# Masked attention with a group norm in front: two visits of each group of heads exchange places

## The chip, the cores and the metric

The kernel runs on one core of a Trainium2 chip. The metric is the device time of one launch in microseconds (us). The kernel before takes 1812.58 us, the median of three runs (1812.48, 1812.58 and 1813.05).

Engine names are those of the profile: PE is the matrix engine and PEld its weight loads, ACT the scalar engine, DVE the vector engine, POOL the GpSimd engine, SP the engine that only issues transfers here.

## The reference

`x` is 32 images of 256 channels and 32 x 32 pixels, float32. Each image goes through a group norm (32 groups of 8 channels), is projected to queries, keys and values (1x1 convolutions, that is, products with 256 x 256 weights), and attends over its own 1024 pixels with 8 heads of 32 channels. A pixel sees only the pixels before it (the diagonal is masked too). The input is added at the end.

```python
xf = _gn(x).reshape(B, C, S)                       # B=32, C=256, S=1024
q = jnp.einsum('oc,bcs->bos', q_w, xf) + q_b[None, :, None]
kv = jnp.einsum('oc,bcs->bos', kv_w, xf) + kv_b[None, :, None]
...
mask = jnp.tril(jnp.ones((S, S), dtype=x.dtype), -int(MASK_CENTER))
scores = jnp.einsum('bhqd,bhkd->bhqk', q, k) / jnp.sqrt(jnp.asarray(dk, x.dtype))
scores = jnp.where(mask == 0, jnp.asarray(-10000.0, x.dtype), scores)
attn = jax.nn.softmax(scores, axis=-1)
attn = jnp.where(mask == 0, jnp.asarray(0.0, x.dtype), attn)
out = jnp.einsum('bhqk,bhkd->bhqd', attn, v)
return x + out
```

## The kernel before, in words

**Visits.** The 1024 keys are eight blocks of 128, and so are the queries. The scores stand with keys on the partitions and queries along the row. The blocks at or below the diagonal (36 of 64) are worked off in six *visits* for each group of four heads; an image has two groups (`NG` = 2), so twelve visits, and the launch has 32 x 12 = 384 of them. `VISITS` (L557) says what a visit makes. Its long part goes to a tile `e` of 128 x 4 heads x 512, its short part to a tile `eh`. A short part is either a `pair` (the two diagonal blocks of two neighbouring key blocks, packed into 192 columns a head) or a plain piece of 256 columns (`full`). Visits 0, 1, 3 and 5 have a pair, visits 2 and 4 a plain piece. Visit 4 is the *visit of three pieces*: a long part of 384 and 128 columns, a short one of 256. Visit 5 has a long part of 512 columns and the diagonal pair of key blocks 4 and 5, which is `pair(2, 0)`.

**One turn of the loop (L705 to L722).** Turn i issues `scores` of visit i (L339), then what is listed for the turn in `at` (a projection of the next image, as a rule), then `values` of visit i-1 (L399), `add_keys` of visit i-1 (L421), and then what is listed in `after`. The order of the instructions on each engine is the order in which this code issues them (`manual_schedule`); an engine takes them strictly one after the other, and semaphores hold an instruction back until its inputs are there. The numbers of turns below are those inside an image, 0 to 11.

- `scores`: PE makes the score products (L302) into three double banks of PSUM. ACT takes the exponentials: two calls for `e` (L384), then one for `eh` (L380). If the visit is in `PAIRS`, `mask` (L320) is called at once: two `affine_select` on POOL (L330) turn the pair in `eh` into two masked squares in the tile `diagonal`, of which there is one for the first two pairs (tag "D", 0) and one for the last two ("D", 1).
- `values`: PE multiplies the exponentials with the values (L409), by the list `PRODUCTS` (L568). A product that reads "D" needs the mask of its pair. After the last visit of a half (visits 1 and 5) ACT copies the sum out (L418).
- `add_keys`: DVE adds the tiles of exponentials into one, by the list `ADDS` (L583), at L427. The sum of the second half is gathered in the long tile of visit 2 (`TOTAL`).

**What else goes by turns.** `PREPARE` (L624) spreads the norm of the next image over turns; for b of 2 and more it is called with the first visit of image b, so the offsets -12 to -3 fall in the image before. In turn 3 stand `norm_mean` (PE L162 into `pm`, ACT L185) and `norm_deviation`: three tiny `tensor_tensor` on DVE of 2 elements a partition each (L195, L196, L197), which make `dev`. In turn 4, after `values` and `add_keys`, stand `norm_variance` (PE: eight small products `pv` of `avg` and `dev`, L162; ACT: L209) and `norm_rstd` (POOL: L217, L219). `norm_apply` on ACT (L235) follows in turns 5, 6, 7 and 9.

`SUMS` (L625) has the folds of the summed exponentials: `fold` (L436) adds half of the partitions onto the other half, by a transfer that POOL issues (L440), in turns 3 and 5 for the first sum, 7 and 9 for the second, 10 and 12 (turn 0 of the next image) for the third, 13 and 15 for the fourth. `stack` (L442, SP) collects them, `sum_folded` (L448), `invert` (L485) and `finish` (L521) come an image later on DVE and SP.

**Buffers.** The tag "e" has four buffers, which the tiles take in turn: long tiles of visits 0, 1, 3, the second diagonal tile (made in visit 3), then those of visits 4 and 5. The tag "eh" has three. `acc` of PSUM has one.

**The last image** has no projection beside it and is not folded. `sums` (L466) adds the keys up on PE with a matrix of ones (`pd`, L461), by the list `SUMMED` (L595). Where a visit of the last image is in `SUMMED` (other than visit 1), `add_keys` is left out for it. At the very end PE makes the sums of visit 11 and its values, and DVE inverts and finishes in two halves (`end_last`, L536).

Of the kernel before, what the change touches and what calls it, by code (L numbers as in the profile page):

```python
# [17 lines left out]
P = 128  # L18
# [14 lines left out]
def tile_norm_attention_residual(  # L33
# [20 lines left out]
    B, C, H, W = x.shape  # L54
# [44 lines left out]
    def unshifted():  # L99
# [178 lines left out]
        def full(kb, first, width, at):  # L278

            return at, width, [[(c, kb, first, width, slice(at, at + width))] for c in (0, KEYS)]  # L280

        def pair(j, at):


            even, odd = 2 * j, 2 * j + 1
            c0, c1, c2, c3 = (at + n * KEYS for n in range(4))
            return at, 3 * KEYS, [
                [
                    (0, even, even * P, P, slice(c1, c3)),
                    (0, odd, odd * P, KEYS, slice(c0, c1)),  # L290
                ],
                [
                    (KEYS, odd, odd * P, P, slice(c0, c2)),
                    (KEYS, even, even * P + KEYS, KEYS, slice(c2, c3)),
                ],
            ]
# [23 lines left out]
        def mask(b, g, raw, j):  # L320


            hf, place = j // 2, (2 * j % 4) * P
            if ("e", b, g, "D", hf) not in live:
                live["e", b, g, "D", hf] = epool.tile(
                    [P, 4, HALF], F32, tag=("e0", "e")[hf], bufs=4, name=f"diagonal_{b}_{g}_{hf}"
                )
            square = live["e", b, g, "D", hf]
            for s in range(2):
                nc.gpsimd.affine_select(  # L330
                    out=square[:, :, place + s * P : place + (s + 1) * P],
                    in_=raw[:, :, (1 - s) * KEYS : (3 - s) * KEYS],
                    pattern=[[0, 4], [(1, -1)[s], P]], compare_op=ALU.is_gt, fill=0.0, base=0,
                    channel_multiplier=(-1, 1)[s],
                )
            if j == 0:
                nc.gpsimd.memset(square[0:1, :, 0:1], 1.0)

        def scores(b, v):  # L339
# [27 lines left out]
            for ins in first:  # L367
                tc.declare_no_dep(wait.ins, ins.ins, reason="the semaphore orders them")
            made = short_of((0, 1), *rest if i in PAIRS else ())
            if i not in PAIRS:  # L370
                for f in rest:
# [19 lines left out]
            live["e", b, g, "L", i], live["e", b, g, "H", i] = e, eh  # L391
            if i in PAIRS:
                mask(b, g, eh, PAIRS[i])

# [141 lines left out]
        def end_last(b):  # L536
# [4 lines left out]
            for part in both:  # L541
# [13 lines left out]
        Q = lambda a, b: slice(a * P, b * P)  # L555
# [3 lines left out]
            ([full(1, 2 * P, 4 * P, 0)], [pair(1, 0)]),  # L559
            ([full(0, 4 * P, 4 * P, 0)], [full(1, 6 * P, 2 * P, 0)]),  # L560
            ([full(2, 4 * P, 4 * P, 0)], [pair(3, 0)]),
            ([full(4, 5 * P, 3 * P, 0), full(6, 7 * P, P, 3 * P)], [full(5, 6 * P, 2 * P, 0)]),
            ([full(3, 4 * P, 4 * P, 0)], [pair(2, 0)]),
        ]
        N, TOTAL = NG * len(VISITS), 2
        PAIRS = {0: 0, 1: 1, 3: 3, 5: 2}

        PRODUCTS = [  # L568
            (0, [
# [3 lines left out]
            (0, [(("L", 1, Q(0, 2)), 1, Q(2, 4)), (("D", 0, Q(2, 3)), 2, Q(2, 3)), (("D", 0, Q(3, 4)), 3, Q(3, 4))]),  # L573
            (1, [(("L", 2, Q(0, 4)), 0, Q(0, 4)), (("L", 1, Q(2, 4)), 1, Q(0, 2)), (("H", 2, Q(0, 2)), 1, Q(2, 4))]),
            (1, [(("L", 3, Q(0, 4)), 2, Q(0, 4)), (("D", 1, Q(2, 3)), 6, Q(2, 3)), (("D", 1, Q(3, 4)), 7, Q(3, 4))]),
            (1, [
                (("L", 4, Q(0, 3)), 4, Q(1, 4)), (("L", 4, Q(3, 4)), 6, Q(3, 4)), (("H", 4, Q(0, 2)), 5, Q(2, 4)),
            ]),
            (1, [(("L", 5, Q(0, 4)), 3, Q(0, 4)), (("D", 1, Q(0, 1)), 4, Q(0, 1)), (("D", 1, Q(1, 2)), 5, Q(1, 2))]),
        ]  # L580
        FIRST, LAST = (0, 2), (1, 5)

# [2 lines left out]
            [(("D", 0, Q(1, 4)), ("L", 0, Q(0, 3))), (("D", 0, Q(2, 4)), ("L", 1, Q(0, 2)))],  # L585
            [(("L", 2, Q(0, 2)), ("L", 1, Q(2, 4))), (("L", 2, Q(2, 4)), ("H", 2, Q(0, 2)))],
            [(("L", 2, Q(0, 4)), ("L", 3, Q(0, 4)))],
            [
                (("L", 2, Q(1, 4)), ("L", 4, Q(0, 3))), (("L", 2, Q(3, 4)), ("L", 4, Q(3, 4))),
                (("L", 2, Q(2, 4)), ("H", 4, Q(0, 2))),  # L590
            ],
            [(("L", 2, Q(0, 4)), ("D", 1, Q(0, 4))), (("L", 2, Q(0, 4)), ("L", 5, Q(0, 4)))],
        ]

        SUMMED = {  # L595
            1: [(("D", 0, Q(0, 4)), Q(0, 4))],
            5: [(("L", 2, Q(0, 4)), Q(0, 4)), (("L", 5, Q(0, 4)), Q(0, 4)), (("D", 1, Q(0, 4)), Q(0, 4))],
            7: [(("D", 0, Q(0, 4)), Q(0, 4)), (("L", 0, Q(0, 3)), Q(1, 4)), (("L", 1, Q(0, 2)), Q(2, 4))],
            9: [(("L", 2, Q(0, 4)), Q(0, 4)), (("L", 3, Q(0, 4)), Q(0, 4))],
            10: [  # L600
                (("L", 4, Q(0, 3)), Q(1, 4)), (("L", 4, Q(3, 4)), Q(3, 4)), (("H", 4, Q(0, 2)), Q(2, 4)),
                (("D", 1, Q(2, 4)), Q(2, 4)),
            ],
            11: [(("L", 5, Q(0, 4)), Q(0, 4)), (("D", 1, Q(0, 2)), Q(0, 2))],
        }
        at, after = {}, {}

# [124 lines left out]
    def shifted():  # L732


        with ExitStack() as inner:
# [34 lines left out]
            with tc.For_i(0, B, 1) as b:  # L770
# [93 lines left out]
                )  # L864

    outside = unshifted()
    again = nc.values_load(outside[0:1, 0:1], min_val=0, max_val=P)
    with tc.If(again > 0):
# [26 lines left out]
```

## Time and profile before

| what | value |
|---|---|
| median of three runs | 1812.58 us |
| the profiled execution | 1813.86 us |
| its span, first to last instruction | 1812.2 us |
| busy: PE, DVE, ACT, POOL | 1797.5, 1643.0, 1457.2, 919.4 us |
| mean granted clock of PE | 0.999 |
| score products L302, 18432 of them | 584.9 us busy |
| value products L409 from `e` and `diagonal` (4608 and 4096 of them) | 401.8 and 160.4 us busy |
| `affine_select` L330, 512 of them | 649.1 us busy, 1291 ns mean |
| additions `e<-e,diagonal` of 2048 elements, L427, 62 of them | 142.1 us busy, 2293 ns mean |

A row of the view of groups gives line, engine, operation, tiles, shapes and count, then busy time and the mean duration of one, then the idle time of the engine just before them and what ended it. In the timeline a row has start and duration in us from the span's beginning, and in square brackets the idle time before it with its releaser. In the list of waits the figures are us in total, times, and the longest.

An image takes about 55.45 us in the steady part: the starts of the first score products of images 5 and 6 differ by that, as those of most other neighbours do.

### The profile page before, as it was taken

The page shows a single profiled execution, that of the slowest core. Times are in us where ns is not written, and L with a number is a line of the kernel's source. Part 1 is how long each engine was busy: PE and PEld are TensorE (multiplying, and loading weights), DVE is VectorE, ACT ScalarE, POOL GpSimd, SP SyncE. Part 2 cuts the span into 40 slices and gives each one's busy share as a digit, 9 for nine tenths or more (in the row PEclk, how much of TensorE's full clock was granted, in tenths as well). Part 3 has the DMA queues.
Part 4 walks back from the last instruction along what each step waited for, and adds up shares of the span by engine and source line. Part 5 has one row for each costly group of instructions (what it writes and reads, how often), then busy time and mean ns, then how long its engine had stood idle before and what let it go on. Part 6 is the DMA issues. An engine that isn't in the chain of part 4 may idle for free.

```text
span 1812.2 us, 81732 instructions
## 1 busy us (share of the span) xinstructions
PE 1797.5 (99%) x37036; PEld 956.9 (53%) x37036; DVE 1643.0 (91%) x1832; ACT 1457.2 (80%) x1985; POOL 919.4 (51%) x901
## 2 busy tenths in 40 slices
PE   9999999999999999999999999999999999999997
PEld 5555555555555555555555555555555555555553
DVE  4689999999999999999999999999999999999987
ACT  6888878888778888788887888887888878888774
POOL 2345555545545555455555455554554555555532
PEclk9999999999999999999999999999999999999999
DMA  3457676776766766766767667677667676675653
GB/s 124 72 96 142 130 138 124 137 149 130 147 118 137 145 131 139 133 132 133 148 135 146 111 137 153 125 142 132 136 132 147 132 140 122 134 156 121 124 113 85
DMA packets 86531, 236.78 MB, mean 131 GB/s; under 512 B 21280, under 2 KB 22304, under 8 KB 70304
## 3 DMA queue, kind: packets, MB, share of 16 engines
q0 software_dynamic: 15872, 97.53, 35.8%
q1 hardware_dynamic: 70304, 133.96, 28.2%
q8 instruction: 290, 4.75, 1.1%
q14 instruction: 65, 0.53, 0.1%
HBM read 66.85 MB, written 34.57 MB: 56 GB/s over the span
## 4 chain that ended last, share of the span: by engine, by line
PE 98%; DVE 1%; ACT 0%; issue 0%; DMA 0%; POOL 0%; DVEq 0%
PE sT L302 30%; PE acc L409 27%; PE pp L162 26%; PE ppv L162 13%; PE pd L461 0%; ACT e L384 0%; PE pv L162 0%; DMA x<-in_x_dram 0%; DVE diagonal L427 0%; DVE st L177 0%; DVE e L427 0%; PE pm L162 0%; POOL diagonal L330 0%; ACT eh L380 0%; DVE rb_last L528 0%
## 5 line engine op out<-in xcount | busy, mean ns | idle before, releaser
L330 POOL TENSOR_SCALAR_AFFINE_SELECT diagonal<-eh 128x512 f32<-128x512 f32 x512 | 649.1, 1291 | 748.6 <-ACT eh L380 748.4
L384 ACT ACTIVATE e<-sT 128x1024 f32<-128x1024 f32 x768 | 745.2, 1022 | 260.7 <-PE sT L302 256.7
L302 PE MATMUL sT<-q,k 32*64 32x128 f32 (+2 forms) x18432 | 584.9, 372 | 0.5 <-issue 0.3
L427 DVE TENSOR_TENSOR e<-e,e 128x1024 f32<-128x1024 f32 x315 | 553.6, 1757 | 21.6 <-ACT v L266 4.8
L302 PEld LDWEIGHTS sT<-q,k 32*64 32x64 f32 x18432 | 405.4, 131 | 181.4 <-PE sT L302 59.3
L162 PE MATMUL pp<-xn,wT 128*32 128x512 f32 x4096 | 493.3, 598 | 0.6 <-issue 0.3
L409 PE MATMUL acc<-e,v 128*32 128x384 f32 (+3 forms) x4608 | 401.8, 450 | 0.0
L380 ACT ACTIVATE eh<-sT 128x768 f32<-128x768 f32 (+1 forms) x384 | 340.9, 888 | 0.0
L409 PEld LDWEIGHTS acc<-e,v 128*32 128x32 f32 x4608 | 149.7, 110 | 261.0 <-issue 238.0
L162 PE MATMUL ppv<-wT,xn 128*32 128x256 f32 x4096 | 247.5, 382 | 0.0
L162 PEld LDWEIGHTS pp<-xn,wT 128*32 128x32 f32 x4096 | 107.8, 109 | 200.1 <-issue 165.9
L427 DVE TENSOR_TENSOR diagonal<-diagonal,e 128x1536 f32<-128x1536 f32 x126 | 188.4, 1495 | 16.8 <-PE acc L409 9.1
L427 DVE TENSOR_TENSOR e<-e,eh 128x1024 f32<-128x1024 f32 x127 | 176.0, 1386 | 6.9 <-DVE e L427 0.5
L427 DVE TENSOR_TENSOR e<-e,diagonal 128x2048 f32<-128x2048 f32 x62 | 142.1, 2293 | 39.2 <-POOL diagonal L330 36.2
L409 PEld LDWEIGHTS acc<-diagonal,v 128*32 128x32 f32 x4096 | 119.6, 110 | 92.9 <-issue 75.7
L162 PEld LDWEIGHTS ppv<-wT,xn 128*32 128x32 f32 x4096 | 120.4, 109 | 79.6 <-issue 7.2
L409 PE MATMUL acc<-diagonal,v 128*32 128x128 f32 x4096 | 160.4, 273 | 0.0
L235 ACT ACTIVATE xn<-x,shift,rstd 128x256 f32<-128x256 f32 x248 | 137.1, 613 | 0.0
L440 POOL DMA_DIRECT2D e<-e x124 | 102.3, 825 | 38.1 <-PE pp L162 31.1
L528 DVE SCALAR_TENSOR_TENSOR rb<-num,v_bias_col,x 128x256 f32<-128x256 f32 x248 | 117.5, 514 | 4.4
L440 POOL DMA_DIRECT2D diagonal<-diagonal x124 | 119.4, 963 | 0.0
L526 DVE TENSOR_TENSOR num<-num,rb 128x512 f32<-128x512 f32 x124 | 110.8, 894 | 0.0
(78 smaller groups left out, 1004.4 us busy)
## 6 DMA issues: line engine op xcount, KB each, us to landing
diagonal<-diagonal POOLq DMA_DIRECT2D x62, 512.0 KB, 8.3
e<-e POOLq DMA_DIRECT2D x62, 512.0 KB, 5.2
rb<-inverses SPq DMA_DIRECT2D x124, 256.0 KB, 4.7
out_dram<-rb SPq DMA_DIRECT2D x124, 256.0 KB, 5.1
x<-in_x_dram SPq DMA_DIRECT2D x120, 256.0 KB, 6.2
diagonal<-diagonal POOLq DMA_DIRECT2D x62, 256.0 KB, 4.9
folded<-diagonal SPq DMA_DIRECT2D x62, 256.0 KB, 4.4
e<-e POOLq DMA_DIRECT2D x62, 256.0 KB, 5.1
```

The costliest lines, as they stand in the source:

```text
L162: nc.tensor.matmul(out[part], lhsT=lhsT[:, part], rhs=rhs, start=start, stop=stop, skip_group_check=True)
L235: nc.scalar.activation(to, of, AF.Identity, bias=live["shift", b][:, g : g + 1], scale=rstd)
L302: return nc.tensor.matmul(bank[c : c + KEYS, cols], lhsT=live["k", b, g][rows, kb * P + c : kb * P + c + KEYS], rhs=live["q", b, g][rows, ...
L330: nc.gpsimd.affine_select(out=square[:, :, place + s * P : place + (s + 1) * P], in_=raw[:, :, (1 - s) * KEYS : (3 - s) * KEYS], pattern=[ ...
L380: exp = nc.scalar.activation(eh.rearrange("p (n bank) q -> p bank n q", n=2)[:, :, :, :narrow], short[:, :, :, :narrow], AF.Exp)
L384: nc.scalar.activation(e[:, 2 * a : 2 * a + 2, :wide], pairs[a][:, :, :wide], AF.Exp)
L409: nc.tensor.matmul(acc[HD * j : HD * (j + 1), of], lhsT=live["v", b][:, kb, h * HD : (h + 1) * HD], rhs=e[:, j, :], start=first, stop=last ...
L427: nc.vector.tensor_add(to, to, tile_of(b, g, at))
L440: nc.gpsimd.dma_start(out=total[:rows], in_=total[rows : 2 * rows], accum_op=ALU.add)
L526: nc.vector.tensor_mul(num, num, rb)
L528: nc.vector.scalar_tensor_tensor(blocks(rb, s), blocks(num, s, s == 1), v_bias_col[:, g : g + 1], blocks(xt[:, g, cols], s), ALU.add, ALU.add,
```

## The change

The last two entries of `VISITS` exchange places. The pair of key blocks 4 and 5 (with the 512 columns of key block 3) becomes visit 4, the visit of three pieces becomes visit 5. The lists that go by visit follow: `PAIRS`, `PRODUCTS`, `ADDS` and `SUMMED`. `LAST`, `TOTAL`, `PREPARE`, `SUMS` and all other lists of turns stay as they are.

```diff
             ([full(2, 4 * P, 4 * P, 0)], [pair(3, 0)]),
+            ([full(3, 4 * P, 4 * P, 0)], [pair(2, 0)]),
             ([full(4, 5 * P, 3 * P, 0), full(6, 7 * P, P, 3 * P)], [full(5, 6 * P, 2 * P, 0)]),
-            ([full(3, 4 * P, 4 * P, 0)], [pair(2, 0)]),
         ]
...
-        PAIRS = {0: 0, 1: 1, 3: 3, 5: 2}
+        PAIRS = {0: 0, 1: 1, 3: 3, 4: 2}
...
+            (1, [(("L", 4, Q(0, 4)), 3, Q(0, 4)), (("D", 1, Q(0, 1)), 4, Q(0, 1)), (("D", 1, Q(1, 2)), 5, Q(1, 2))]),
             (1, [
-                (("L", 4, Q(0, 3)), 4, Q(1, 4)), (("L", 4, Q(3, 4)), 6, Q(3, 4)), (("H", 4, Q(0, 2)), 5, Q(2, 4)),
+                (("L", 5, Q(0, 3)), 4, Q(1, 4)), (("L", 5, Q(3, 4)), 6, Q(3, 4)), (("H", 5, Q(0, 2)), 5, Q(2, 4)),
             ]),
-            (1, [(("L", 5, Q(0, 4)), 3, Q(0, 4)), (("D", 1, Q(0, 1)), 4, Q(0, 1)), (("D", 1, Q(1, 2)), 5, Q(1, 2))]),
...
+            [(("L", 2, Q(0, 4)), ("D", 1, Q(0, 4))), (("L", 2, Q(0, 4)), ("L", 4, Q(0, 4)))],
             [
-                (("L", 2, Q(1, 4)), ("L", 4, Q(0, 3))), (("L", 2, Q(3, 4)), ("L", 4, Q(3, 4))),
-                (("L", 2, Q(2, 4)), ("H", 4, Q(0, 2))),
+                (("L", 2, Q(1, 4)), ("L", 5, Q(0, 3))), (("L", 2, Q(3, 4)), ("L", 5, Q(3, 4))),
+                (("L", 2, Q(2, 4)), ("H", 5, Q(0, 2))),
             ],
-            [(("L", 2, Q(0, 4)), ("D", 1, Q(0, 4))), (("L", 2, Q(0, 4)), ("L", 5, Q(0, 4)))],
...
-            5: [(("L", 2, Q(0, 4)), Q(0, 4)), (("L", 5, Q(0, 4)), Q(0, 4)), (("D", 1, Q(0, 4)), Q(0, 4))],
+            5: [
+                (("L", 2, Q(0, 4)), Q(0, 4)), (("L", 5, Q(0, 3)), Q(1, 4)), (("L", 5, Q(3, 4)), Q(3, 4)),
+                (("H", 5, Q(0, 2)), Q(2, 4)),
+            ],
...
-            10: [
-                (("L", 4, Q(0, 3)), Q(1, 4)), (("L", 4, Q(3, 4)), Q(3, 4)), (("H", 4, Q(0, 2)), Q(2, 4)),
-                (("D", 1, Q(2, 4)), Q(2, 4)),
-            ],
-            11: [(("L", 5, Q(0, 4)), Q(0, 4)), (("D", 1, Q(0, 2)), Q(0, 2))],
+            10: [(("L", 4, Q(0, 4)), Q(0, 4)), (("D", 1, Q(0, 4)), Q(0, 4))],
+            11: [(("L", 5, Q(0, 3)), Q(1, 4)), (("L", 5, Q(3, 4)), Q(3, 4)), (("H", 5, Q(0, 2)), Q(2, 4))],
```

## The prediction, made before the changed kernel was built

> **What bounds the kernel now.** I read the page first, then the list of waits, then the timeline of one image, engine by engine.
>
> ```profile
> span 1812.2 us, 81732 instructions
> ...
> PE 1797.5 (99%) x37036; PEld 956.9 (53%) x37036; DVE 1643.0 (91%) x1832; ACT 1457.2 (80%) x1985; POOL 919.4 (51%) x901
> ...
> PE 98%; DVE 1%; ACT 0%; issue 0%; DMA 0%; POOL 0%; DVEq 0%
> ```
>
> PE is busy for 99% of the span and carries 98% of the chain that ended last. So the time changes only where a PE product starts earlier or later. But the end of a matmul in the records is modelled, so a short wait of PE can hide inside "busy". I therefore measured starts, not busy time. The list of waits has two of the places where PE depends on other engines:
>
> ```profile
> PEld acc L409 <- POOL diagonal L337: 5.6, 28, 0.3
> ...
> PE pv L162 <- DVE dev L197: 0.6, 2, 0.4
> ```
>
> The first is turn 7: the values of visit 6 wait for the mask of its pair (the memset at L337 comes behind both selects). From the first product of `acc` to the next score product takes 1.548 us in 28 images, and 1.413 in images 0, 1 and 24, where the mask is early: 0.135 us each. The second is what matters here. Turn 4 of image 20 on PE:
>
> ```profile
> 1147.75 1.55 PE L302 MATMUL sT<-q,k 32*64 32x256 f32 x48
> 1149.23 1.93 PE L162 MATMUL ppv<-wT,xn 128*32 128x256 f32 x32
> 1150.98 1.04 PE L409 MATMUL acc<-e,v 128*32 128x512 f32 x8
> 1151.84 0.62 PE L409 MATMUL acc<-diagonal,v 128*32 128x128 f32 x16
> 1152.33 0.24 PE L162 MATMUL pv<-dev,avg 128*32 128x2 f32 x8
> 1152.50 1.47 PE L302 MATMUL sT<-q,k 32*64 32x128 f32 x48
> ```
>
> and DVE in the same place:
>
> ```profile
> 1150.50 1.21 DVE L427 TENSOR_TENSOR e<-e,eh 128x1024 f32<-128x1024 f32 x1
> 1151.64 0.15 DVE L195 TENSOR_TENSOR dev<-mv,mean 128x2 f32<-128x2 f32 x1
> 1151.82 0.16 DVE L196 TENSOR_TENSOR dev<-dev 128x2 f32<-128x2 f32 x1
> 1152.02 0.16 DVE L197 TENSOR_TENSOR dev<-dev,mv 128x2 f32<-128x2 f32 x1
> 1152.09 2.29 DVE L427 TENSOR_TENSOR e<-e,e 128x2048 f32<-128x2048 f32 x1
> ```
>
> `dev` is ready at 1152.18, `pv` starts 0.147 us later, and this 0.147 is the same in images 2 to 30: PE is waiting for DVE there, in 29 images. It costs nothing yet. In image 1 `dev` is done 1.9 us early, and `pv` starts 4.575 us after the turn began; in the others it is 4.58. So the slack is zero, and every delay of `dev` stops PE, with scores, projections and values of all later turns queued behind it.
>
> **The skill.** "SBUF — State Buffer", section "SBUF: two separate sides", says that DVE and GpSimd share a pair of ports under an exclusive lock: a DVE operation with two SBUF inputs and a GpSimd operation exclude each other, and the loser waits for the whole instruction of the other. The trace agrees, even for the smallest operation. In image 0 two selects meet the same `dev`:
>
> ```profile
> 27.15 1.67 POOL L330 TENSOR_SCALAR_AFFINE_SELECT diagonal<-eh 128x512 f32<-128x512 f32 x2 [5.55 <-ACT eh L380]
> ```
>
> ```profile
> 27.35 0.98 DVE L427 TENSOR_TENSOR e<-e 128x512 f32<-128x512 f32 x1 [12.20 <-PE acc L409]
> 28.25 0.58 DVE L195 TENSOR_TENSOR dev<-mv,mean 128x2 f32<-128x2 f32 x1
> 28.87 0.16 DVE L196 TENSOR_TENSOR dev<-dev 128x2 f32<-128x2 f32 x1
> ```
>
> L195, 147 ns elsewhere, takes 584 and ends with the second select (28.82). The two sides also alternate: select 1, addition, select 2, L195. A select takes 0.63 us alone and ends about 0.49 us after a lock it waited for. "Perfetto Trace Analysis", section "Tensor Engine Instruction (MATMUL, LD_WEIGHTS)", says that the end of a PE instruction is estimated and its start observed; the `pv` wait above, with no gap shown on PE, is such a case.
>
> **The change, part by part.** PE's work in an image is the same: 768 columns of values in both exchanged visits (1.408 us each), 1.403 us for the scores of a pair visit, 1.481 for three pieces. Turns 4 and 10 become 0.078 shorter, 5 and 11 as much longer. ACT's exponential of the short part (0.82 us for a pair, 1.03 for three pieces) moves by one visit; ACT is ready by the next scores in both orders. The DVE additions of turns 5 and 6 exchange (2 x 2048 against 1536 + 512 + 1024 elements). Each of these is hidden, and costs nothing unless a step below says so.
>
> *Step 1, the moved mask.* In turn 5 the exponential of the pair ends 3.85 us into the turn, and the first select starts at 3.92 (1156.42, turn from 1152.50). In turn 4 the same sequence will put it at 1147.75 + 3.92 = 1151.67. That is between L195 (1151.64) and L196 (1151.82), while the addition in front still holds the ports until 1151.71. POOL is free there (its last issue ends at 2.58 us of the turn). If L195 goes first, select 1 holds the ports to about 1152.28, L196 ends there, select 2, queued since then, to 1152.77, and L197 ends with it or just behind: 0.60 us late. If select 1 goes first (1151.71 to 1152.20), L195 slips in behind it, select 2 ends at 1152.70, then L196 and L197 to 1152.90: 0.72 late. I take the middle, 0.66. Bounds: 0 if all three `dev` operations get in before a select, 0.32 if L197 slips in between the two selects, 0.95 if each of the selects finds nobody and runs its full 0.63 with the gaps of DVE behind it. `pv` starts by the same amount later. The 0.078 that PE saves in the scores of turn 4 is lost, since `pv` waits; the 0.078 more in turn 5 is paid. So 0.74 us an image, 29 images: +21.5. Behind `pv` wait all of PE, ACT's L209, POOL's L217 and the norm; none of these is late by more than `pv` itself.
>
> *Step 2, the wait of turn 7 goes.* Both selects of visit 6 now meet two additions of 2048 (2.29 us) on DVE: 2.10 and 2.68 us for the two. After the change they meet 1536, 512 and 1024 (nominally 1.75, 0.69, 1.23). DVE reaches the 1536 about 3.4 us into turn 6; select 1 waits from 3.94 to its end (5.15), is done at 5.65, the 512 comes to 6.2, select 2 to 6.7, so 2.05 us into turn 7, where it is needed at 4.0. What is late next there is PE itself. 28 x 0.135: -3.8.
>
> *Step 3, the second group.* In turn 10 the mask queues behind the second fold on POOL (issue to 4.2 us) and an addition of 2048; DVE's next addition needs the mask and waits about 1 us. It must be back in step at turn 1, where its addition at L427 waits for PE at 4.11 us and DVE is free at 3.50. I find it free at about 3.85: 0, with an upper bound of 0.3 us an image. The fold of the third sum is issued some 3 us later, lands 8.3 us after that, before its successor at 2.5 us of turn 1: 0.
>
> *Step 4, the end.* The sums of turn 7 of the last image lose 256 of 1536 columns (1778.04 to 1780.72: 2.68 us in all): -0.43. The last sum no longer waits for a mask:
>
> ```profile
> 1798.70 1.04 PE L461 MATMUL pd<-e,pick 128*32 128x512 f32 x8
> 1800.00 0.64 PE L461 MATMUL pd<-diagonal,pick 128*32 128x256 f32 x8 [0.26 <-POOL diagonal L330]
> ```
>
> Without it the second row would start 0.87 after the first, 0.43 earlier; DVE, which goes on from there, had been idle for 0.42: -0.42.
>
> Sum: 21.5 - 3.8 - 0.43 - 0.42 = +16.8 us. The profiled execution was 1813.86 us (span 1812.2 and 1.7 around it), 0.07% above the median of 1812.58; the median plus the sum is 1829.4.
>
> **The rivals.**
> - *One select in between* (L197 before select 2): 0.40 x 29 = 11.6, sum +7.0, 1819.5 us. For it: L197 follows L196 by 0.04 us only. Against: in every meeting that I looked at, the waiting side got the ports next.
> - *No collision, on the other side*: the three tiny operations run through, and the selects come behind. Then turn 4 pays 0.078 x 29 = 2.3, and the rest stays: -2.3, 1810.3 us; if `dev` came another 0.08 earlier, 1808.0. It decides at 1152.18: a first select that gets the ports only after this harms nobody. For it: L195 is issued 0.03 before the select. Against: gaps of 0.03 between dependent operations, in which POOL already waits, and image 0.
> - *DVE out of step as well*: step 3 comes out at its upper bound, DVE is late at turn 1 by 0.3 us and with it `dev`: 28 x 0.3 = 8.4, about 1838 us. For it: DVE is 91% busy. Against: the free 0.6 us at turn 1.
> - *No effect where it was meant*, the wait at turn 7 stays since DVE is late by the delay of `pv`: 3.8 more, inside the range.
>
> **How the numbers follow.** Both selects in between 0.50, one 0.20, none 0.17, out of step 0.13. Range 1815 to 1841: it holds the first, the second and the fourth case. About 0.2%, 3.6 us, is what a measurement of this kernel can tell from no change. "None" gives -2.3 to -4.6, so I split it: faster 0.06, same 0.11, slower 0.83.
>
> **What would show it.** In the changed profile `pv` should start about 5.2 us after turn 4 began, 0.147 behind L197; L195 or L196 should last some 0.5 us and end with a select; the image should take about 56.05 us; the row of `acc` waiting for L337 should be gone, and the wait of `pd` for L330 too. If L195 to L197 keep their 0.15 us in all images, step 1 is wrong, and the time is below 1812. If `pv` is on time and the kernel is slower all the same, the cause is one that I have not named.

## The result, and the profile after

The changed kernel takes 1833.27 us, the median of four runs (1830.86 to 1834.68); the kernel before, beside it on the same chip, 1812.56 (1812.48 to 1813.05). The ratio is 1.0112, with a 95% interval of 1.0095 to 1.013. It is slower, by 20.7 us; 1829.4 had been predicted, with a range of 1815 to 1841. The profiled execution took 1833.38 us.

The head of the page after, with the chain that ended last by engine:

```profile
span 1831.7 us, 81670 instructions
...
PE 1798.4 (98%) x37036; PEld 961.7 (53%) x37036; DVE 1667.8 (91%) x1831; ACT 1454.9 (79%) x1985; POOL 780.6 (43%) x901
...
PE 93%; DVE 6%; issue 1%; ACT 0%; POOL 0%; DVEq 0%; POOLq 0%
```

The span grew by 19.5 us, and PE's busy time by 0.9 only: PE now stands still. The chain passes through DVE for 6% of the span instead of 1%. In the list of waits (us in total, times, longest), the row of `pv` has grown from 0.6 us:

```profile
DVE e L427 <- POOL diagonal L330: 36.8, 33, 1.1
...
PE pv L162 <- DVE dev L197: 16.4, 27, 1.1
```

The row of `acc` waiting for L337 is gone, as is that of `pd` waiting for L330. The first row here, DVE waiting for the mask of the second group, is not a new loss: in the kernel before it has 36.2 us, also in 33 waits. The exchange only moved it. 31 of these waits now fall in turn 11 by PE's count; before, they fell in turn 0 of the next image. No turn of PE is longer for it.

Turn 4 of image 20 of the changed kernel, on PE:

```profile
1158.68 1.48 PE L302 MATMUL sT<-q,k 32*64 32x128 f32 x48
1160.09 1.93 PE L162 MATMUL ppv<-wT,xn 128*32 128x256 f32 x32
1161.84 1.04 PE L409 MATMUL acc<-e,v 128*32 128x512 f32 x8
1162.70 0.62 PE L409 MATMUL acc<-diagonal,v 128*32 128x128 f32 x16
1163.98 0.24 PE L162 MATMUL pv<-dev,avg 128*32 128x2 f32 x8 [0.66 <-DVE dev L197]
```

on DVE:

```profile
1161.39 1.21 DVE L427 TENSOR_TENSOR e<-e,eh 128x1024 f32<-128x1024 f32 x1
1162.52 0.15 DVE L195 TENSOR_TENSOR dev<-mv,mean 128x2 f32<-128x2 f32 x1
1162.70 0.55 DVE L196 TENSOR_TENSOR dev<-dev 128x2 f32<-128x2 f32 x1
1163.29 0.55 DVE L197 TENSOR_TENSOR dev<-dev,mv 128x2 f32<-128x2 f32 x1
1163.76 2.28 DVE L427 TENSOR_TENSOR e<-e,e 128x2048 f32<-128x2048 f32 x1
```

and on POOL:

```profile
1162.61 1.22 POOL L330 TENSOR_SCALAR_AFFINE_SELECT diagonal<-eh 128x512 f32<-128x512 f32 x2 [1.39 <-ACT eh L380]
```

L195 still runs free. The first select starts 3.93 us into the turn, L196 waits for it and lasts 0.55 us instead of 0.16; the second select is queued meanwhile, and L197 waits for that one. `pv` starts 5.30 us into the turn, 0.14 behind the end of L197; before, it was 4.58. This isn't one image. The view by tile gives minimum, median and maximum over the launch (ns):

```profile
L196 DVE TENSOR_TENSOR dev<-dev x32: 160/547/554, 8.5 to 1728.0; 128x2 f32<-128x2 f32 x32
L197 DVE TENSOR_TENSOR dev<-dev,mv x32: 161/552/554, 8.7 to 1728.6; 128x2 f32<-128x2 f32 x32
L195 DVE TENSOR_TENSOR dev<-mv,mean x31: 146/149/585, 28.4 to 1727.8; 128x2 f32<-128x2 f32 x31
```

To see where the 19.5 us lie, I took the start of the first score product of each turn, and the median over images 2 to 30 of the distance to the next. Seven of the twelve turns are the same in both kernels to 0.001 us. The five others:

| us | turn 4 | turn 5 | turn 7 | turn 10 | turn 11 | all twelve |
|---|---|---|---|---|---|---|
| before | 4.753 | 4.552 | 4.692 | 4.630 | 4.563 | 55.449 |
| after | 5.476 | 4.630 | 4.558 | 4.552 | 4.640 | 56.114 |
| difference | +0.723 | +0.078 | -0.134 | -0.078 | +0.077 | +0.665 |

29 times 0.665 is 19.3. What images 2 to 30 last beyond 29 such medians, in single pauses of PE, is 4.6 us after and 3.4 before: +1.2. The last image is 1.0 shorter. These make the 19.5.

Below, the sum of the twelve medians is called the *steady image*, and the time beyond 29 of them *pauses*. All times below are of runs at a granted clock of 0.995 or more; one of the seven runs of the kernel with only the second group exchanged had 0.702, took 2424.36 us, and is left out.

### The profile page after: what moved, and what is told of

It is laid out like the page before. It is cut to its first block, busy times and chain, and to the rows that moved or that the text cites. A ratio compares the mean times of both kernels' runs of the same rounds, so it can differ in the third digit from the quotient of the medians.

```text
span 1831.7 us, 81670 instructions
## 1 busy us (share of the span) xinstructions
PE 1798.4 (98%) x37036; PEld 961.7 (53%) x37036; DVE 1667.8 (91%) x1831; ACT 1454.9 (79%) x1985; POOL 780.6 (43%) x901
## 3 DMA queue, kind: packets, MB, share of 16 engines
q8 instruction: 290, 4.75, 1.1%
## 4 chain that ended last, share of the span: by engine, by line
PE 93%; DVE 6%; issue 1%; ACT 0%; POOL 0%; DVEq 0%; POOLq 0%
PE sT L302 30%; PE pp L162 26%; PE acc L409 25%; PE ppv L162 10%; DVE e L427 3%; DVE dev L196 1%; DVE dev L197 1%; PE pd L461 1%; PE pv L162 0%; PE busy L148 0%; DVE rb L533 0%; ACT e L384 0%; DVE diagonal L427 0%; DVE dev L195 0%; PE pm L162 0%
## 5 line engine op out<-in xcount | busy, mean ns | idle before, releaser
L330 POOL TENSOR_SCALAR_AFFINE_SELECT diagonal<-eh 128x512 f32<-128x512 f32 x512 | 515.2, 1028 | 892.0 <-ACT eh L380 892.0
L409 PE MATMUL acc<-e,v 128*32 128x512 f32 (+3 forms) x4608 | 403.5, 450 | 0.0
L427 DVE TENSOR_TENSOR e<-e,eh 128x1024 f32<-128x1024 f32 x126 | 181.5, 1441 | 6.8 <-ACT xn L235 0.5
L440 POOL DMA_DIRECT2D diagonal<-diagonal x124 | 111.5, 899 | 64.3 <-DMA diagonal<-diagonal 64.3
```

Of the source, the lines that this page charges most:

```text
L330: nc.gpsimd.affine_select(out=square[:, :, place + s * P : place + (s + 1) * P], in_=raw[:, :, (1 - s) * KEYS : (3 - s) * KEYS], pattern=[ ...
L409: nc.tensor.matmul(acc[HD * j : HD * (j + 1), of], lhsT=live["v", b][:, kb, h * HD : (h + 1) * HD], rhs=e[:, j, :], start=first, stop=last ...
L427: nc.vector.tensor_add(to, to, tile_of(b, g, at))
L440: nc.gpsimd.dma_start(out=total[:rows], in_=total[rows : 2 * rows], accum_op=ALU.add)
```

## The experiments

The eleven kernels ran in three groups, each group on one chip and beside the kernel before, whose median there was 1814.2 to 1814.3 us (1812.0 to 1817.5). Ratios are to it; they and their intervals are estimates over the runs, not quotients of the medians.

| run | us, median (range) | ratio, 95% interval | profiled execution | steady image | pauses |
|---|---|---|---|---|---|
| first group only exchanged | 1839.19 (1834.95 to 1840.51) | 1.0137, 1.0121 to 1.0152 | 1834.95 | 56.115 | 5.5 |
| second group only | 1820.50 (1811.95 to 1822.25) | 1.0021, 1.0006 to 1.0037 | 1822.25 | 55.390 | 13.6 |
| `dev` ahead of the additions | 1818.40 (1815.65 to 1821.81) | 1.0025, 1.0019 to 1.0032 | 1817.80 | 55.380 | 10.3 |
| `dev` on ACT | 1811.99 (1806.57 to 1815.07) | 0.9979, 0.997 to 0.9988 | 1811.99 | 55.270 | 8.2 |
| before + two selects on `e` | 1835.71 (1835.35 to 1835.79) | 1.0117, 1.0102 to 1.0132 | 1835.72 | 56.266 | 1.9 |
| before + two selects on `eh` | 1834.38 (1832.58 to 1837.87) | 1.0112, 1.0098 to 1.0127 | 1834.90 | 56.203 | 1.9 |
| second group, earlier fold | 1824.45 (1820.37 to 1834.46) | 1.006, 1.004 to 1.008 | 1829.10 | 55.394 | 20.0 |
| `dev` on ACT, earlier fold | 1838.11 (1833.52 to 1849.64) | 1.0137, 1.0113 to 1.0161 | 1838.86 | 56.168 | 7.7 |
| first group, `dev` on ACT | 1837.01 (1832.47 to 1847.63) | 1.0132, 1.0108 to 1.0156 | 1837.53 | 56.194 | 5.8 |
| before, `dev` on ACT | 1823.55 (1820.48 to 1828.16) | 1.0053, 1.0038 to 1.0068 | 1824.45 | 55.641 | 8.2 |
| second group, no stores | 1809.06 (1808.62 to 1809.69) | 0.997, 0.9959 to 0.9981 | 1809.18 | 55.408 | 1.1 |

The last two columns are read from the profiled execution alone. Executions of one kernel differ by up to 16 us, and a profiled one can be far from typical: with the first group only it is the fastest of four, with the second group only the slowest of six.

### One group alone

The five lists were made per group of heads, and one group kept the old order.

```diff
-            longs, shorts = VISITS[i]
+            longs, shorts = VISITS[g][i]
...
-            if i in PAIRS:
-                mask(b, g, eh, PAIRS[i])
+            if i in PAIRS[g]:
+                mask(b, g, eh, PAIRS[g][i])
```

> The two visits exchange places in the first group of heads alone (visits 4 and 5); the second group keeps the order of before. Theory (the selects of the moved mask come between the three dev operations of turn 4, and pv with all of PE waits 0.72 us in 29 images): the loss stays whole, turn 4 takes 5.48 us, an image 56.11, about 1833.5 us. Rival A (the second group pays: the mask of turn 10 behind a fold on POOL, DVE waiting for it, late at turn 1): the loss goes for the most part, below 1818 us. Rival B (PE itself pays for the new order of its products, in either group): about half of the 20.7 us, near 1823.

> The exchange in the second group alone (visits 10 and 11). Theory: no dev operation near turn 10, so no loss; turn 7 keeps its wait of 0.135 us; 1812.0 to 1812.6 us, image 55.45. Rival A (second group): close to 1833. Rival B (PE's own order): near 1823.

With the first group exchanged the steady image is 56.115, with 5.476 in turn 4 and 4.558 in turn 7: the whole steady loss of the change lies here, and the gain at turn 7 too. The median lies 5.7 us above the 1833.5 that had been expected; the one execution with a trace, the fastest, has 5.0 us of pauses in turn 0. With the second group alone turn 4 is 4.749 and turn 7 still 4.637, so the steady image is 0.06 below before, worth 1.7 us. The kernel is slower all the same, by pauses of 6.5 us in turn 4 and 6.8 in turn 5. I had not foreseen these (the kernel before has 0.3 and 0.0 there); the last experiments below deal with them.

### The three small operations elsewhere

In the changed kernel, L195 to L197 go ahead of the two additions of visit 2 on DVE:

```diff
-                    if b < B - 1 or v not in SUMMED or v == 1:
+                    late = v == 2
+                    if not late and (b < B - 1 or v not in SUMMED or v == 1):
                         add_keys(b, v)
...
+                if i and late:
+                    add_keys(b, v)
```

> The changed kernel, with one thing reordered on DVE: in turn 3 the three dev operations are issued ahead of the two additions of visit 2 and not behind them. Theory: dev is done about 2.2 us into turn 4, before the selects come at 3.92; pv starts at PE's own time, 4.50; turn 4 takes 4.67, turn 7 keeps its 4.56, an image about 55.31; 1808.4 us (1807.8 to 1809.5), faster than both kernels. Rivals A and B: dev matters little, 1825 to 1834 us. Danger for the theory's number: the selects meet longer additions, end near 3.1 us of turn 5, and the scale of the norm behind them may reach ACT late; then turn 5 or 6 gets longer by some tenths.

or leave DVE for ACT, as two activations for each group, one for the offset, one for its square plus the variance:

```diff
...
-                nc.vector.tensor_add(dev, mv[:, :, 0], minus_mean)
+                for g in range(NG):
+                    nc.scalar.activation(off[:, g : g + 1], mv[:, g, 0:1], AF.Identity, bias=minus_mean[:, g : g + 1])
+                for g in range(NG):
+                    nc.scalar.activation(
+                        dev[:, g : g + 1], off[:, g : g + 1], AF.Identity, bias=mv[:, g, 1:2], scale=off[:, g : g + 1],
+                    )
...
+                return
```

> The changed kernel with dev computed on ACT by four tiny activations in turn 4 (ACT is idle there from 0.34 to 1.19 us), none on DVE. Theory: no dev operation can meet a select; dev is ready near 1.2 us, pv at PE's own 4.50, image about 55.31, 1808.4 us (1807.8 to 1810). Rivals A and B: 1825 to 1834 us.

The exchange and its masks are in both, and only the meeting is gone. Turn 4 falls from 5.476 to 4.605 and 4.632, that is by 0.87 and 0.84. That is the 0.72 which the exchange had lost there, and 0.15 and 0.12 more. The rest comes mostly of the exchange, which could not show its gain while `pv` waited for the selects: the scores of turn 4 are 0.08 shorter, and ACT, whose exponential of a pair is shorter than that of three pieces, ends its copy of `v` (L266) earlier. `pv` waits for this copy too. In the kernel before the copy ends 4.52 us into turn 4 and `pv` starts 0.057 behind it, so that two waits end there together, that for `dev` and that for the copy; with `dev` on ACT the copy ends at 4.41, and `pv` starts 0.053 behind it.

Both kernels had been expected at 1808.4 us with an image of 55.31. The images come near this, but the pauses keep both above it; with `dev` ahead of the additions the median of turn 0 is also longer, 4.782 instead of 4.645. On ACT an image is 0.18 us shorter than before, worth 5.2 us in 29; the pauses (8.2 us, against 3.4 in the profile of before) give 4.8 of it back. The result, 1811.99 us, is 0.2% below the kernel before, and is the fastest of those that compute everything.

### Two selects in the kernel before, and nothing else

If two selects in the middle of `dev` are enough, the order of visits isn't needed for the loss. In turn 4 two selects that keep every element were added behind the exponentials of visit 4, on its long tile or on its short one, which is ready later.

```diff
             if i in PAIRS:
                 mask(b, g, eh, PAIRS[i])
+            if (g, i) == (0, 4):
+                for s in range(2):
+                    same = e[:, :, s * P : (s + 1) * P]
+                    nc.gpsimd.affine_select(
+                        out=same, in_=same, pattern=[[0, 4], [0, P]], compare_op=ALU.is_gt, fill=0.0, base=1,
+                        channel_multiplier=0,
+                    )
```

> The kernel before, order of visits untouched, with two more selects of 512 elements a partition on POOL in turn 4, which keep every element of a part of the long tile of visit 4 as it is; they can start when the second exponential is done, 3.1 us into the turn, while DVE still adds (until 3.97). Theory (selects between the dev operations stop PE): select 1, L195, select 2, L196, L197 or the like, dev at about 5.15 us, pv at about 5.3 instead of 4.58, turn 4 takes about 5.48, an image 56.17, ratio to before 1.0115 to 1.0125. Rivals A and B (order of visits, second group): nothing is exchanged, so ratio 1.000 to 1.002.

> As the run before, but the two selects work on the short tile of visit 4 and so start about 4.11 us into the turn, behind L195 (3.89) and L196 (4.07) and ahead of L197 (4.27). Theory: only L197 meets the first select and ends with it near 4.75; pv at about 4.90, turn 4 takes about 5.08, an image 55.77, ratio 1.0045 to 1.006. If the selects cost PE in another way than through dev, the loss is the same as in the run before (ratio near 1.012).

On `e`, image 20, DVE and then PE:

```profile
1167.14 0.59 DVE L195 TENSOR_TENSOR dev<-mv,mean 128x2 f32<-128x2 f32 x1
1167.77 0.55 DVE L196 TENSOR_TENSOR dev<-dev 128x2 f32<-128x2 f32 x1
1168.35 0.16 DVE L197 TENSOR_TENSOR dev<-dev,mv 128x2 f32<-128x2 f32 x1
```

```profile
1168.66 0.24 PE L162 MATMUL pv<-dev,avg 128*32 128x2 f32 x8 [0.70 <-DVE dev L197]
```

The selects come a little earlier, so L195 and L196 are the two that wait, and turn 4 is 5.575. On `eh` they come later, and only L197 waits:

```profile
1165.09 0.15 DVE L195 TENSOR_TENSOR dev<-mv,mean 128x2 f32<-128x2 f32 x1
1165.27 0.16 DVE L196 TENSOR_TENSOR dev<-dev 128x2 f32<-128x2 f32 x1
1165.47 0.50 DVE L197 TENSOR_TENSOR dev<-dev,mv 128x2 f32<-128x2 f32 x1
1165.88 2.28 DVE L434 TENSOR_TENSOR e<-e,e 128x2048 f32<-128x2048 f32 x1
```

Turn 4 is 5.082 there. So the loss depends on which of the three operations meets a select: one caught costs 0.33 us, two cost 0.82, and the moved mask, which also catches two, 0.72.

The second of these kernels is nevertheless as slow as the first, which I hadn't expected. POOL and PE of the same image show why (the selects added are L397, those of the masks L330):

```profile
1165.32 3.34 POOL L397 TENSOR_SCALAR_AFFINE_SELECT eh<-eh 128x512 f32<-128x512 f32 x2 [1.53 <-ACT eh L380]
1168.63 1.15 POOL L217 TENSOR_TENSOR rstd<-rstd,power 128x2 f32<-128x2 f32 x1
1169.86 0.31 POOL L219 TENSOR_TENSOR shift<-mean,rstd 128x2 f32<-128x2 f32 x1
1170.20 3.11 POOL L330 TENSOR_SCALAR_AFFINE_SELECT diagonal<-eh 128x512 f32<-128x512 f32 x2
```

```profile
1180.02 0.64 PE L416 MATMUL acc<-diagonal,v 128*32 128x128 f32 x16 [0.35 <-POOL diagonal L337]
```

The second select found the addition of 2048 elements in the ports, so the pair lasts 3.34 us instead of the 1.22 of the changed kernel. POOL is late for all that follows, and turn 7, where PE waits for a mask anyway, grows from 4.692 to 5.118.

### The pauses: a fold moved, then the stores left out

With the exchange in the second group, the first fold of the third sum comes 2.7 us later on POOL, in turn 11 instead of 10. If that alone made the pauses of turns 4 and 5, issuing it a turn earlier should end them:

```diff
-                        when(v, lambda b=b, n=n: fold(b, n, 2 * HD), after)
+                        when(v - (n == 2), lambda b=b, n=n: fold(b, n, 2 * HD), after)
```

> The exchange in the second group alone, and the first fold of the third sum issued on POOL ahead of the moved mask of turn 10 (in the list of turn 9) and not behind it. The exchange in the second group alone had a steady image of 55.39 to 55.50 us, like before, but 10 to 13 us of single pauses of PE in turns 4 and 5, which end 2.2 to 2.4 us after an instruction fetch began. Theory C (the pauses come from the fold that is issued 2.7 us later and so falls together with other transfers): with the fold in its old place the pauses go back to 2 to 5 us, ratio 0.999 to 1.001. Rival D (pauses depend on how the stream of instructions falls into fetches, not on the fold): they stay, ratio 1.002 to 1.006.

> The changed kernel with dev on ACT and the first fold of the third sum issued ahead of the mask of turn 10. The run with dev on ACT alone had an image of 55.27 us and some 8 us of single pauses. Theory C: the pauses go down to 2 to 5 us, the image stays at 55.27, ratio to before 0.995 to 0.9975. Rival D: as without it, ratio 0.997 to 0.999.

So the fold alone is not what makes them, and neither kernel became faster. In the first of the two, turns 4 and 5 keep 5.6 and 5.9 us of pauses, and those of turn 0 grow from 0.9 to 9.2. In the second they do fall (0.4 and 0.6, from 2.9 and 1.5), but PE stands still in turn 0 of nearly every image: its median goes from 4.645 to 5.551. In the list of waits of that kernel the score products now stand still without a releaser:

```profile
PE sT L310 <- issue: 18.2, 22, 2.2
```

The next two tried where turn 0 gets into trouble: `dev` on ACT with the first group alone, and in the kernel before (edits as above).

> The exchange in the first group alone, with dev on ACT. Theory: the gain of turn 7 stays (4.56), turn 4 takes 4.63 as in the run with dev on ACT in both groups, turns 10 and 11 are those of before, so an image of 55.27 us against 55.45; the transfers of the third sum keep the place of before, so few single pauses of PE in turns 4 and 5. Ratio 0.996 to 0.998, some 5 us below before, if pauses are as many as in before.

> The kernel before with dev on ACT, nothing exchanged. Theory: dev did not cost PE anything before (pv starts 4.58 us into turn 4 with it and 4.575 without), so turn 4 stays within 0.05 us of 4.75, the wait of turn 7 stays, an image of 55.40 to 55.45, ratio 0.998 to 1.001. If dev on DVE was itself a cost of the kernel before, the ratio is near that of the exchanged kernel with dev on ACT (0.997).

Both miss the time. The first has 4.620 in turn 4 and 4.557 in turn 7, as expected, but 5.580 in turn 0. The second misses its turns as well. It loses the wait of turn 7 (4.558; the mask on POOL is done 0.34 us earlier), has 4.889 in turn 0 and 7.8 us of pauses there, and its turn 4 is 4.836 and not 4.75. Its list of waits says why:

```profile
PEld pv L162 <- ACT v L274: 6.6, 30, 0.2
```

The four activations put off ACT's exponentials by 0.13 us, its copy of `v` ends at 4.61 instead of 4.52, and `pv` waits for that. So in the order of before, taking `dev` off DVE gains nothing at `pv`.

What comes ahead of the end of such a pause is a transfer that belongs to PE itself. Turn 4 of image 15 of the kernel with only the second group exchanged, on PEld:

```profile
874.51 0.14 PEld L162 LDWEIGHTS ppv<-wT,xn 128*32 128x32 f32 x4 [0.20 <-issue]
875.72 1.22 PEld L162 LDWEIGHTS ppv<-wT,xn 128*32 128x32 f32 x26 [1.06 <-issue]
```

and its transfers of the ten microseconds to 878 us, by queue (packets, MB, share of the 16 engines):

```profile
q0 software_dynamic: 91, 0.58, 49.5%
q1 hardware_dynamic: 327, 0.68, 24.1%
q8 instruction: 1, 0.02, 0.5%
```

Queue q8 carries instructions, 16 KB in a packet; every page here has 290 or 291 such packets. They are PE's by their number: the 4.75 MB of the queue are 64 bytes for each of the 74072 instructions of PE and PEld, and all the others together have 7660 in the record of the kernel before. This packet starts at 873.3 us, 0.3 us into the turn, and the pause ends 2.4 us later. In this kernel all ten pauses of PEld in images 2 to 30 that are longer than 0.55 us and have no releaser end 2.16 to 2.42 us after the start of such a packet; the twelve of `dev` on ACT in the kernel before, all in turn 0, end 2.3 to 2.6 us after one. The next table has, for each half microsecond around the start of turn 4, the share of it in which such a packet is under way, as a mean over images 4 to 29:

```
us from turn 4     -3.0 -2.5 -2.0 -1.5 -1.0 -0.5  0.0  0.5
before              .03  .24  .65  .59  .25  .12  .00  .00
second group only   .00  .04  .22  .35  .33  .34  .36  .22
no stores           .32  .82  .69  .14  .04  .00  .00  .00
```

The folds and stores fill the transfer engines until about 1 us ahead of the turn, and with the second group exchanged this traffic is spread later (between 1.0 and 0.5 us ahead of it, folds and stores keep the engines 43% busy, against 16% before). The theory is that the packet with instructions waits behind it, and that PE meanwhile runs dry, that is, has no instruction left to start. So in the last run the stores of the first three output quarters of all images but the last were left out (these outputs are computed, but not written):

```diff
-            nc.sync.dma_start(out=x_out[b, :, g, cols], in_=rb)
+            if b == B - 1 or n == 3:
+                nc.sync.dma_start(out=x_out[b, :, g, cols], in_=rb)
```

> The exchange in the second group alone, and the stores of the first three quarters of the output left out for all images but the last (so three of four quarters of the output are not written; what is computed stays). These stores are issued in turns 2 and 4 and fill the transfer engines between 3.5 and 1 us ahead of turn 4. Theory E (PE's instruction fetches wait behind bulk transfers and PE runs dry in turns 4 and 5): the fetch ahead of turn 4 comes early again, the pauses of turns 4 and 5 (13 us in the exchange of the second group alone) go below 4 us, an image stays at 55.39 to 55.45, ratio 0.997 to 1.0005. Rival D (the pauses depend on how the stream of instructions falls into fetches): they stay at 8 to 13 us, ratio 1.002 to 1.006.

The pauses of turns 4 and 5 are gone (0.0 us each; 1.1 in all), and the packet comes 1 to 2 us earlier (last line above). The steady image stays (55.408), and the edit takes nothing from PE's instructions, which speaks against rival D. Score products in the two pages, with the stores and without:

```profile
L302 PE MATMUL sT<-q,k 32*64 32x128 f32 (+2 forms) x18432 | 587.0, 372 | 1.4 <-issue 1.1
```

```profile
L302 PE MATMUL sT<-q,k 32*64 32x128 f32 (+2 forms) x18432 | 583.7, 372 | 0.2
```

The profiled executions of the two kernels are 13.1 us apart, of which 12.5 are pauses (13.6 less 1.1); the medians are 11.4 apart. That bulk transfers near these fetches make the pauses is shown for turns 4 and 5; that they do it by holding up the packet fits the times given, and no run held up a packet in another way. For turn 0 the packet also runs later (mostly from -1.0 to 1.0 us in the two kernels with 0.9 us more in the median, -1.5 to -0.5 before), but no run took traffic away there; that cause is likely and was not tried. Which order keeps both places free stays open.

## Why the prediction was right

**What bounds the kernel, and the point without slack.** Right. The 0.147 us between L197 and `pv` in the kernel before was the sign that `dev` had no slack, though PE showed hardly any idle time there. One wait was not named: where `dev` is early, `pv` waits for ACT's copy of `v`, which ends almost together with it. The 4.575 us of image 1 are this wait and not PE's own time. It hides no loss, since a later `dev` costs its whole delay all the same. The two selects added to the kernel before make the same loss without any exchange.

**Step 1, the moved mask.** Right in mechanism, and the likeliest of the cases. The order is the first of the two named there: L195, select 1, L196, select 2, L197. The term for the delay of `dev` was too small: 0.66 had been taken, the middle of 0.60 and 0.72, and it is 0.72. The figure behind the 0.60 was wrong here. A select that waited for the lock was put at 0.49 us. In the timeline above the two take 1.22 together: the second ends 0.58 after L196, and L197 ends with it. With the 0.078 of turn 5 an image loses 0.80 instead of 0.74, and 29 images 23.2 instead of 21.5. What the Trainium skill says in "SBUF — State Buffer", section "SBUF: two separate sides", of the lock on the ports, agrees with the trace down to two elements a partition: 0.15 us become 0.55.

**Step 2, the wait of turn 7.** Right: -0.134 an image where -0.135 stood, and its row is gone. It comes with the exchange in the first group: 4.558 in turn 7 there, 4.637 with the second group only.

**Step 3, the second group.** The steady times are as predicted: turns 10 and 11 exchange 0.078, turns 0 to 3 stay, and DVE is in step. That the later transfers cost nothing was right only for the data. For PE's own instructions they cost pauses, for which the prediction has no term: 13.6 us in the profiled execution with the second group exchanged alone, against 3.4 before. In the full change only 4.6 appear, 4.1 of them in turns 4 and 5; PE waits for `dev` in turn 4 anyway, which can cover such a pause (not shown). Where that wait is removed, with `dev` on ACT, 8.2 us of pauses appear.

**Step 4, the end.** The sums of turn 7 fell by 0.42, as worked out. The last sum no longer waits:

```profile
1818.30 1.05 PE L461 MATMUL pd<-e,pick 128*32 128x384 f32 x16
1819.17 0.61 PE L461 MATMUL pd<-eh,pick 128*32 128x256 f32 x8
```

The second row starts 0.87 after the first, as predicted, and DVE's last operations come 0.40 earlier. But the span didn't get this: SP's last wait took 2.63 us instead of 2.24. In its place a single pause of 0.5 us in the last image of the kernel before happens to be missing after.

**The sum.** 16.8 had been predicted for the profiled execution and 19.5 came. Step 1 gave 1.7 more, and the pauses 1.2, for which the prediction had no term. The range of 1815 to 1841 held three of its four cases, so that the time fell into it says little; it is the timeline of turn 4 that tells the first case from the others.

**The rivals.** One select in between fell (L196 and L197 are both caught; the kernel with the late selects on `eh` shows what its turn 4 would have been, 5.08). No collision fell: L196 and L197 have medians of 547 and 552 ns. DVE out of step fell, since turn 1 and turn 3 have the same medians in both kernels.

## What to carry to other kernels

Before moving an instruction on an engine that shares ports with another, look up what runs on the other engine at the very time where it will land, and whether PE waits for it: the size of the operation that is hit says nothing of the price, since it pays for the whole of the other one. Where PE is the bound, compare starts from turn to turn, because a wait that costs nothing yet shows no idle time. And count PE's instructions among the transfers: if a change lets bulk traffic run until PE's next block is due, PE can run dry, with no semaphore to show why.

## What the runs showed of the hardware

- The Trainium skill, "Runtime: NRT & Kernel Launch", section "Instruction fetch mechanics", says that instructions come in blocks of 16 KiB over a queue of the engine's own, and that this is mostly hidden. The traces agree on the block. How well it is hidden depended here on when other traffic falls: the pauses of turns 4 and 5 were 0.3 us in the kernel before, 13.2 us with the second group exchanged, and 0.0 with that and most stores left out. Single ones in turn 0 of other kernels lasted up to 2.2 us.
- An operation on two elements, 0.15 us alone, takes 0.50 to 0.59 when a select of 512 holds the ports. In the other direction, a select of 0.63 us lasted 2.76 when an addition of 2048 elements went first (it is the second of the two that take 3.34 together).
